# A four-layer graph network on one core: two small products after each group of four tiles in the first and fourth layer

## The chip, the cores and the metric

The kernel runs on one core of a Trainium2 chip. The metric is the device time of the whole kernel in microseconds. TensorE (PE in the profile, its weight loads PEld) multiplies matrices into PSUM; VectorE (DVE) and ScalarE (ACT) work on SBUF and PSUM; GpSimd (POOL) issues here almost only indirect DMAs, that is gathers of rows by index; SyncE (SP) issues the plain loads. The engines run side by side and wait for each other through semaphores.

## The reference

There are 12,500 nodes with 32 features and 400,000 edges, sorted by their destination. Each of four layers normalises the nodes, passes a message along each edge, sums the messages at the nodes and adds that to the features. The change touches the first layer (with a degree count of the third layer, which the kernel computes beside it) and the fourth:

```python
# first layer
m = relu(node_feat[src] + edge_feat)
neigh = segment_sum(m, dst)
return (1 + eps) * node_feat + neigh

# third layer's degree, counted beside the first
deg = segment_sum(ones(E), src)

# fourth layer
h = relu(edge_scalars @ fc_w1) * sqrt2
w = (h @ fc_w2).reshape(E, 4, 8, 8)          # 256 weights for each edge
x = node_features[src]
s1, v1, s2, v2 = x[:, :8], x[:, 8:].reshape(E, 8, 3), edge_sh[:, 0], edge_sh[:, 1:4]
out_s = A * (einsum('eu,euw->ew', s1 * s2, w[:, 0]) + c * einsum('eui,ei,euw->ew', v1, v2, w[:, 1]))
out_v = B * (einsum('eu,euw,ei->ewi', s1, w[:, 2], v2) + einsum('eui,euw->ewi', v1 * s2, w[:, 3]))
node_out = segment_sum(concat(out_s, out_v), dst)
```

## The kernel before

Edges are cut into tiles of 128. Four tiles (G = 4) make a group, four groups a chunk of 2048 edges (CT = 16 tiles), and there are 196 chunks, so 784 groups a layer. All loops over chunks are unrolled. A host-side check of the destinations (the flag `fast`) chooses between two programs; with these inputs the fast one runs, and only that one is spoken of here. The Tile framework places the semaphores: a tile of a pool with `bufs=n` waits until all that used the tile n before it in that pool has ended. It also sets each engine's order, so that an engine's instructions need not stand in the order of the source.

**First layer** (`layer0`, run by `edges`). For each group, POOL gathers four times 128 source rows (`gather`, L535), four groups ahead of their use, into six buffers `hs`. DVE adds the edge features (L663), ACT applies the relu (L664). Then `tail` does two things. `collect` builds a one-hot matrix of the destinations (DVE, L457) and multiplies it with the messages into one PSUM tile for the chunk (`ps_win`, PE, L460, f32: each product is two records in the profile); at the chunk's end ACT copies it out (L463) and stores it. And the degree is counted: the source index is split into a high and a low digit (DVE, L680 to L683), both become one-hot matrices `ohi` and `olo` in bf16 (DVE, L687, two buffers each), and PE multiplies them into `ps_deg` (L690, four products a group); at the chunk's end DVE adds that to `deg` (L693). DVE and ACT run their instructions in order, so a wait at L693 or L463 holds all that follows.

**Fourth layer** (`edges3`). Chunks are again pipelined. `gather` (POOL, L1274) fetches 16 times 128 rows a chunk, into four buffers `hs`, whose last reader is the multiply into `ps` (L1316) of the chunk's last group. `hidden` (PE, L1285, into the one buffer `ps_h`; ACT, L1287, relu into `hid`) makes the edges' hidden values for the next chunk, a quarter after each group. `product` is called once a group: eight f32 products (16 records) of `hid` with the weights `w2b` into `ps_w` (PE, L1310, two buffers), and then three multiplies on DVE that read `ps_w`: into `pa` (L1314), `ps` (L1316) and `pv` (L1318). Once a chunk DVE reduces them (`outputs`, L1326 to L1334) and splits the result in three bf16 parts with ACT (`thirds`, L472 to L476), PE sums them by one-hot matrices that ACT made (L1340, L1341; `collect`, L1346), and a product with `fold` (L1352) joins the parts.

PSUM pools of the fourth layer: `ps_h` with one buffer of 4 KB a partition, `ps_w` with two of 4 KB, `ps_sum` with one of 2 KB. Of the first: `ps_win` and `ps_deg`, two buffers each.

Of the kernel before, what the change touches and what calls it, by code (L numbers as in the profile page):

```python
# [8 lines left out]
F32 = mybir.dt.float32  # L9
# [5 lines left out]
PSUM = bass.MemoryType.PSUM  # L15

P = 128
D = 32
NP = 125
G = 4  # L20
# [17 lines left out]
def tiles_of(E):  # L38

    C = Q4 * B  # L40
    return E // C * (C // P) - (-(E % C) // P)
# [15 lines left out]
class GNN:  # L57
# [14 lines left out]
    def __init__(self, tc, ctx, a, out, E):  # L72
        self.tc, self.nc, self.ctx, self.a, self.out, self.E = tc, tc.nc, ctx, a, out, E
        self.N = a["x"].shape[0]
        self.J = self.N // NP
        self.T = a["src"].shape[1]
        self.CT = G * CG
        self.IT = self.CT * CPI0
        assert self.N % NP == 0 and self.T % self.IT == 0
        dram = ctx.enter_context(tc.tile_pool(name="dram", bufs=1, space=bass.MemoryType.DRAM))  # L80
        rows = self.N + P
        self.tabs = [
            [dram.tile([rows, D], F32, name=f"acc{l}_{k}", tag=f"acc{l}_{k}") for k in range(NTAB)]
            for l in range(4)
        ]
        self.feats = [dram.tile([rows, D], F32, name=f"feat{l}", tag=f"feat{l}") for l in range(4)]
        self.NW = self.T // self.CT
        self.real = tiles_of(E)


        self.emb8 = dram.tile([9, 8, self.NW, Q4 * B], BF16, name="emb8", tag="emb8")
        self.emb10 = dram.tile([9, 10, self.NW, Q4 * B], BF16, name="emb10", tag="emb10")
        self.mid = dram.tile([rows, D + 1], F32, name="mid", tag="mid")
        self.local = dram.tile([P, self.NW, self.CT + 1], F32, name="local", tag="local")
        self.n_e = dram.tile([P, self.T, 3], F32, name="n_e", tag="n_e")
        self.loc_t = dram.tile([self.NW, Q4 * B], F32, name="loc_t", tag="loc_t")
        self.n_t = dram.tile([4, self.NW, Q4 * B], F32, name="n_t", tag="n_t")
        self.dst_rows = dram.tile([P, self.T], I32, name="dst_rows", tag="dst_rows")
# [367 lines left out]
    def thirds(self, pool, c, step):  # L466
# [8 lines left out]
        else:  # L475
            nc.vector.tensor_tensor(c["f3"][:, :, 2, :], c["f"], c["f3"][:, :, 1, :], op=ALU.subtract)  # L476

    def get(self, pool, l, c):

        c["win"] = pool.tile([P, D], F32, name="win")  # L480
        self.nc.sync.dma_start(c["win"], self.feats[l][ds(self.first(c), P), :])
# [144 lines left out]
    def layer0(self):  # L626
        nc, tc, J = self.nc, self.tc, self.J
        if not self.fast:
            with tc.tile_pool(name="rest", bufs=1) as pool:
                for _ in self.rest(pool):  # L630
                    pass
        with ExitStack() as ctx:
            rest = None
            if self.fast:
                self.resident(ctx)
                rest = self.rest(ctx.enter_context(tc.tile_pool(name="rest", bufs=1)))
                for _ in range(TABS[0]):
                    next(rest)
            big = ctx.enter_context(tc.tile_pool(name="big0", bufs=LEAD + 4 if self.fast else 2))
            gp = ctx.enter_context(tc.tile_pool(name="gather0", bufs=AHEAD + 2))  # L640
            wp = ctx.enter_context(tc.tile_pool(name="work0", bufs=2))
            psum = ctx.enter_context(tc.tile_pool(name="psum0", bufs=2, space=PSUM))
            hist = ctx.enter_context(tc.tile_pool(name="hist0", bufs=2, space=PSUM))

            def load(col):
                if self.fast:
                    c = {"edge_attr_32": self.load(big, "edge_attr_32", col)}
                else:
                    c = {n: self.load(big, n, col) for n in ("src", "dst", "edge_attr_32")}
                    c["row"] = self.load_row(big, "dst_t", col)  # L650
                    c["rows"] = big.tile([P, self.CT], I32, name="rows")
                c["col"] = col
                return c

            def gather(c, t0):
                return self.gather(gp, "hs", 0, c["src"], t0, c)

            def front(c, t0, hs):
                return None

            def main(c, t0, hs, _):
                m = wp.tile([P, G, D], F32, name="m", bufs=3)
                nc.vector.tensor_add(m, hs, c["edge_attr_32"][:, t0 : t0 + G, :])  # L663
                nc.scalar.activation(m, m, AF.Relu)  # L664
                return m

            def tail(c, t0, m):
                if self.fast:
                    self.collect(0, wp, psum, c, m, t0)
                else:  # L670
                    eq = self.same(wp, c["dst"], c["row"], t0)
                    self.firsts(wp, eq, c["dst"], c["rows"], t0)
                    self.scatter(0, wp, psum, eq, m, c["rows"], t0)

                if t0 == 0:
                    c["deg"] = hist.tile([P, P], F32, name="ps_deg")
                hi = wp.tile([P, G], F32, name="hi")
                lo = wp.tile([P, G], F32, name="lo")
                s = c["src"][:, t0 : t0 + G]
                nc.vector.tensor_scalar(hi, s, -0.5 * (J - 1), 1.0 / J, op0=ALU.add, op1=ALU.mult)  # L680
                nc.vector.tensor_scalar_add(hi, hi, ROUND)
                nc.vector.tensor_scalar_add(hi, hi, -ROUND)
                nc.vector.scalar_tensor_tensor(lo, hi, -float(J), s, op0=ALU.mult, op1=ALU.add)  # L683
                ohi = wp.tile([P, G, NP], BF16, name="ohi")
                olo = wp.tile([P, G, J], BF16, name="olo")
                for oh, v, n in ((ohi, hi, NP), (olo, lo, J)):
                    nc.vector.tensor_tensor(oh, self.iota[:, None, :n].to_broadcast([P, G, n]),  # L687
                                            v[:, :, None].to_broadcast([P, G, n]), op=ALU.is_equal)
                for k in range(G):
                    nc.tensor.matmul(c["deg"][:NP, :J], lhsT=ohi[:, k, :], rhs=olo[:, k, :],  # L690
                                     start=t0 + k == 0, stop=t0 + k == self.CT - 1)
                if t0 + G == self.CT:
                    nc.vector.tensor_add(self.deg, self.deg, c["deg"][:NP, :J])  # L693
                    if not self.fast:
                        nc.scalar.dma_start(self.dst_rows[:, ds(c["col"], self.CT)], c["rows"])

            self.edges(load, gather, front, main, tail,
                       windowed=(lambda c, row: c.update(self.places_of(big, row), src=self.sources_of(c))) if self.fast else None, beside=rest)
        with tc.tile_pool(name="end0", bufs=1) as pool:
            agg = self.gather_sum(0, pool)  # L700
            nc.vector.tensor_add(self.x, self.x, agg)
            nc.vector.scalar_tensor_tensor(self.x, self.h, self.eps1, self.x, op0=ALU.mult, op1=ALU.add)
# [549 lines left out]
    def edges3(self):  # L1252

        nc, tc, CT = self.nc, self.tc, self.CT
        with ExitStack() as ctx:
# [3 lines left out]
            ph = ctx.enter_context(tc.tile_pool(name="ph3", bufs=1, space=PSUM))  # L1259
            pw = ctx.enter_context(tc.tile_pool(name="pw3", bufs=2, space=PSUM))  # L1260
            ps = ctx.enter_context(tc.tile_pool(name="ps3", bufs=1, space=PSUM))

            def fetch(c):
                row = c["no"]
# [25 lines left out]
            def scalars(c):  # L1290
# [7 lines left out]
                vv = c["vv"] = wp.tile([P, CT, 3, 8], F32, name="vv")  # L1298
                nc.vector.tensor_mul(vv.rearrange("p g i u -> p g (i u)"), hs[:, :, 8:32], sh[:, :, 0:1].to_broadcast([P, CT, 24]))

            def product(c, g):

                if g == 0:
# [4 lines left out]
                for k in range(4):  # L1308
                    for m in range(2):
                        nc.tensor.matmul(w[:, k, :], lhsT=c["hid"][:, m, 4 * g + k].rearrange("p q s -> p (q s)"), rhs=self.w2b[:, m, :],  # L1310
                                         start=m == 0, stop=m == 1)
                gs = slice(4 * g, 4 * g + 4)
                hs = c["hs"][:, gs, :]
                nc.vector.tensor_mul(c["pa"][:, gs], w[:, :, 0:128].rearrange("p g (w u) -> p g w u", u=16),  # L1314
# [3 lines left out]
                nc.vector.tensor_mul(c["pv"][:, gs].rearrange("p g i (w u) -> p (g i) w u", u=8),  # L1318
                                     w[:, :, None, 192:256].to_broadcast([P, 4, 3, 64]),
                                     c["vv"][:, gs].rearrange("p g i u -> p (g i) u")[:, :, None, :].to_broadcast([P, 12, 8, 8]))  # L1320

            def outputs(c):
                sh = c["sh"]
# [225 lines left out]
```

## Time and profile before

| what | us |
|---|---|
| time, median of 3 runs | 20938.48 (20915.86 to 20953.58) |
| the profiled execution's own time | 20931.77 |
| its span | 20930.0 |
| PE busy | 12599.4 (60%), 56,444 products and as many weight loads |
| DVE busy | 12740.1 (61%) |
| ACT busy | 6408.9 (31%) |
| POOL busy | 14745.9 (70%) |
| gathers of the first layer, from first to last | 72.3 to 4744.6 |
| gathers of the fourth layer, from first to last | 15396.3 to 20767.0 |

The four layers follow each other, with the second and third in one stage between the two that are changed. Busy shares over the whole span therefore mix stages with different limits; each stage has to be read by itself. A product's start in the profile is recorded, its end is modelled. When an instruction waited, the profile names what released it; "issue" is a wait for nothing that it shows, and "remote" one that a semaphore event ended beside which no instruction's end stands. The chain of work that ended last has 27% of the span on DVE, 20% on "issue", 15% on PE, 14% on POOL and 13% on "another core or an unknown queue", the chain's name for "remote".

### The profile page before, as it was taken

How to read it: one execution, taken by the hardware profiler on the slowest of the kernel's cores; microseconds unless marked ns; L12 is line 12 of the kernel's file. 1: busy time of each engine (PE TensorE's matmuls, PEld its weight loads, DVE VectorE, ACT ScalarE, POOL GpSimd, SP SyncE). 2: the span in 40 equal slices, each digit the busy share in tenths (PEclk: the TensorE clock that was granted, in tenths of full speed). 3: DMA queues.
4: the chain of work that ended last, by engine and by line, in shares of the span. 5: the costliest groups of instructions: out<-in, count | busy, mean ns of one | idle time of the engine just before them, and what ended most of it. 6: DMA issues, size and time to landing. Idle time of an engine off the chain costs nothing.

```text
span 20930.0 us, 189759 instructions
## 1 busy us (share of the span) xinstructions
PE 12599.4 (60%) x56444; PEld 6767.2 (32%) x56444; DVE 12740.1 (61%) x25505; ACT 6408.9 (31%) x13844; POOL 14745.9 (70%) x12508
## 2 busy tenths in 40 slices
PE   2443433334766666666666666666637777777776
PEld 2333433331211111111111111111125555555554
DVE  3554444334766666666666666666746666666666
ACT  0001110002333333333333333333324444444444
POOL 5777777774788888888888888888755555555553
PEclk9999999998777777777777777777768888888888
DMA  2113332112444444444444444444411111111111
GB/s 96 46 45 111 113 91 74 23 23 72 98 89 90 88 91 90 89 89 90 90 90 90 90 90 90 90 90 90 92 39 23 23 23 23 23 23 23 23 23 30
DMA packets 1482594, 1406.96 MB, mean 67 GB/s; under 512 B 1055751, under 2 KB 1250897, under 8 KB 1426409
## 3 DMA queue, kind: packets, MB, share of 16 engines
q1 hardware_dynamic: 668550, 1143.45, 17.2%
q0 software_dynamic: 750000, 205.60, 12.0%
q10 hardware_dynamic: 62992, 45.63, 0.7%
q8 instruction: 448, 7.34, 0.1%
q14 instruction: 604, 4.94, 0.1%
HBM read 1156.82 MB, written 236.20 MB: 67 GB/s over the span
## 4 chain that ended last, share of the span: by engine, by line
DVE 27%; issue 20%; PE 15%; POOL 14%; another core or an unknown queue 13%; ACT 7%; DMA 4%; DVEq 0%; ACTq 0%; SPq 0%; POOLq 0%
DVE z L853 6%; POOL acc L1008 5%; POOL hs L809 5%; PE ps_w L1310 5%; POOL hs L535 4%; PE ps_y L850 4%; DVE pv L1318 1%; DMA hs<-feat,src_all 1%; PE ps_o L860 1%; ACT oh L1340 1%; DVE f L1327 1%; DVE pa L1314 1%; ACT X L834 1%; PE ps_sum L1346 1%
## 5 line engine op out<-in xcount | busy, mean ns | idle before, releaser
L1008 POOL DMA_INDIRECT acc<-summed,rows x3125 | 5141.5, 1645 | 999.8 <-issue 882.0
L1274 POOL DMA_INDIRECT hs<-feat,src_all x3125 | 3017.6, 966 | 2462.6 <-DVE ps L1316 1460.3
L535 POOL DMA_INDIRECT hs<-feat,src_all x3125 | 3375.3, 1080 | 1368.4 <-issue 864.4
L809 POOL DMA_INDIRECT hs<-feat,src x3125 | 3210.6, 1027 | 1190.2 <-issue 944.4
L1310 PE MATMUL ps_w<-w2b,hid 128*128 128x256 f32 x12544 | 3194.7, 411 | 68.8 <-issue 53.4
L853 DVE TENSOR_TENSOR z<-ps_y,hid 128x1024 f32<-128x1024 f32 x2352 | 2837.7, 1214 | 411.2 <-PE ps_y L850 161.2
L850 PE MATMUL ps_y<-X,w2t 64*128 64x512 f32 x4704 | 2380.0, 744 | 1132.0 <-DVE z L853 656.2
L1310 PEld LDWEIGHTS ps_w<-w2b,hid 128*128 128x128 f32 x12544 | 2577.7, 209 | 625.8 <-issue 85.8
L850 PE MATMUL ps_y<-Q,w2t 64*128 64x512 f32 x4704 | 1677.6, 838 | 1678.1 <-DVE z L853 1163.8
L460 PE MATMUL ps_win<-m,oh 128*128 128x32 f32 x6272 | 1472.7, 400 | 854.9 <-ACT m L664 211.4
L472 ACT CAST f<-f 128x512 bf16<-128x512 f32 x784 | 481.2, 614 | 4785.3 <-DVE f L878 3878.6
L860 PE MATMUL ps_o<-z,sums 128*32 128x512 f32 x9408 | 1746.1, 700 | 30.0 <-DVE r L865 21.4
L460 PEld LDWEIGHTS ps_win<-m,oh 128*128 128x128 f32 x6272 | 1396.3, 328 | 927.7 <-issue 528.3
L690 PE MATMUL ps_deg<-olo,ohi 128*125 128x100 bf16 x3136 | 462.8, 298 | 2001.6 <-DVE olo L687 1416.9
L1287 ACT ACTIVATE hid<-ps_h 128x1024 f32<-128x1024 f32 x784 | 802.0, 1023 | 2368.0 <-remote 1923.5
L1314 DVE TENSOR_TENSOR pa<-ps_w,q 128x512 f32<-128x512 f32 x784 | 540.1, 689 | 1605.5 <-remote 1407.0
L824 DVE STREAM_TRANSPOSE X<-hs 128x512 f32<-128x512 f32 x392 | 273.4, 700 | 1999.8 <-DMA hs<-feat,src 1328.8
L850 PEld LDWEIGHTS ps_y<-Q,w2t 64*128 64x128 f32 x4704 | 521.2, 256 | 2923.8 <-DVE z L853 1578.9
L850 PEld LDWEIGHTS ps_y<-X,w2t 64*128 64x128 f32 x4704 | 614.2, 210 | 2343.2 <-DVE z L853 1159.5
L663 DVE TENSOR_TENSOR m<-hs,edge_attr 128x128 f32<-128x128 f32 x784 | 228.3, 291 | 1609.6 <-issue 779.8
L664 ACT ACTIVATE m<-m 128x128 f32<-128x128 f32 x784 | 240.3, 310 | 3145.1 <-DVE m L663 1175.9
L690 PEld LDWEIGHTS <-ohi 128*125 128x125 bf16 x3136 | 445.7, 215 | 1990.8 <-DVE ohi L687 1035.7
(207 smaller groups left out, 19667.1 us busy)
## 6 DMA issues: line engine op xcount, KB each, us to landing
has<-loc_t SPq DMA_DIRECT2D x392, 1024.0 KB
srow<-in_src_t SPq DMA_DIRECT2D x392, 512.0 KB
N<-n_t SPq DMA_DIRECT2D x3136, 32.0 KB
hs<-feat,src_all POOLq DMA_INDIRECT x6250
emb<-pp SPq DMA_DIRECT2D x252, 280.0 KB
emb<-emb SPq DMA_DIRECT2D x196, 360.0 KB
emb<-pp SPq DMA_DIRECT2D x252, 224.0 KB
emb<-emb SPq DMA_DIRECT2D x196, 288.0 KB
```

The costliest lines, as they stand in the source:

```text
L460: nc.tensor.matmul(c["sum"], lhsT=oh[:, k, :], rhs=feat[:, k, :], start=t0 + k == 0, stop=t0 + k == self.CT - 1)
L535: self.nc.gpsimd.indirect_dma_start(out=t[:, k, :], out_offset=None, in_=self.feats[l][:], in_offset=bass.IndirectOffsetOnAxis(ap=idx[:, t ...
L690: nc.tensor.matmul(c["deg"][:NP, :J], lhsT=ohi[:, k, :], rhs=olo[:, k, :], start=t0 + k == 0, stop=t0 + k == self.CT - 1)
L809: nc.gpsimd.indirect_dma_start(out=c["hs"][:, k, :], out_offset=None, in_=self.feats[1][:], in_offset=bass.IndirectOffsetOnAxis(ap=c["src" ...
L850: nc.tensor.matmul(y[:, q, :], lhsT=self.w2t[64 * q : 64 * q + 64, h, j, :], rhs=c["Q" if j < 3 else "X"][64 * q : 64 * q + 64, h, :], sta ...
L853: nc.vector.tensor_mul(z, y, c["hid"][:, 2 * h : 2 * h + 2, :])
L860: nc.tensor.matmul(c["o", j // 3][32 * q : 32 * q + 32, :], lhsT=self.sums[:, j, :], rhs=c["z", j, q % 2][:, q // 2, :], start=j % 3 == 0, ...
L1008: nc.gpsimd.indirect_dma_start(out=self.tabs[2][k % NTAB][:], out_offset=bass.IndirectOffsetOnAxis(ap=c["rows"][:, G * g + k : G * g + k + ...
L1274: nc.gpsimd.indirect_dma_start(out=c["hs"][:, k, :], out_offset=None, in_=self.feats[3][:], in_offset=bass.IndirectOffsetOnAxis(ap=c["src" ...
L1287: nc.scalar.activation(c["hid"][:, m, :, 2 * h : 2 * h + 2, :].rearrange("p b q s -> p q b s"), t.rearrange("p q (b s) -> p q b s", s=32), ...
L1310: nc.tensor.matmul(w[:, k, :], lhsT=c["hid"][:, m, 4 * g + k].rearrange("p q s -> p (q s)"), rhs=self.w2b[:, m, :], start=m == 0, stop=m == 1)
L1314: nc.vector.tensor_mul(c["pa"][:, gs], w[:, :, 0:128].rearrange("p g (w u) -> p g w u", u=16), c["q"][:, gs, None, :].to_broadcast([P, 4, ...
```

## The change

A new helper `settle` writes `settles` (2) products into a PSUM pool that has one buffer. Each product takes 128 x 32 weights and one moving column and gives a 32 x 1 result that nothing reads; each is its own tile. It is called once a group:

- in the first layer after the four degree products, with operands that these have just used (`ohi` and `olo` of the group's last tile, bf16);
- in the fourth layer after the group's eight products and ahead of the three multiplies that read them, with operands from `pv` of the group before (f32), which the multiply at L1318 wrote. The first group of the layer has none and no such products.

```diff
@@ -85,6 +85,7 @@
+        self.settles = 2
@@ -475,6 +476,12 @@
+    def settle(self, pool, lhsT, rhs):
+
+        for _ in range(self.settles):
+            t = pool.tile([D, 1], F32, name="ps_t")
+            self.nc.tensor.matmul(t, lhsT=lhsT, rhs=rhs, start=True, stop=True)
+
@@ -641,6 +648,7 @@ layer0
             hist = ctx.enter_context(tc.tile_pool(name="hist0", bufs=2, space=PSUM))
+            after = ctx.enter_context(tc.tile_pool(name="after0", bufs=1, space=PSUM))
@@ -689,6 +697,8 @@ layer0, tail
                     nc.tensor.matmul(c["deg"][:NP, :J], lhsT=ohi[:, k, :], rhs=olo[:, k, :],
                                      start=t0 + k == 0, stop=t0 + k == self.CT - 1)
+                if self.fast:
+                    self.settle(after, ohi[:, G - 1, :D], olo[:, G - 1, 0:1])
@@ -1259,6 +1269,7 @@ edges3
             ps = ctx.enter_context(tc.tile_pool(name="ps3", bufs=1, space=PSUM))
+            after = ctx.enter_context(tc.tile_pool(name="after3", bufs=1, space=PSUM))
@@ -1298,6 +1309,8 @@
+            state = []
+
             def product(c, g):
@@ -1309,6 +1322,8 @@
                         nc.tensor.matmul(w[:, k, :], lhsT=c["hid"][:, m, 4 * g + k].rearrange("p q s -> p (q s)"), rhs=self.w2b[:, m, :],
                                          start=m == 0, stop=m == 1)
+                if state:
+                    self.settle(after, *state)
@@ -1318,6 +1333,7 @@
                 nc.vector.tensor_mul(c["pv"][:, gs].rearrange("p g i (w u) -> p (g i) w u", u=8),
...
+                state[:] = c["pv"][:, 4 * g, 0, 0:D], c["pv"][:, 4 * g, 1, 0:1]
```

## The prediction

> **What bounds the kernel now.** I read the busy time by stage first, with stage edges taken from the first and last gather of each layer. In each row the pairs are busy time and instruction count of PE, PEld, DVE, ACT and POOL, then granted clock, DMA share, GB/s.
>
> ```profile
> 72.00:4780.00 4708.00, 1845.00 (x9408) 1783.08 (x9408) 2060.01 (x6784) 389.08 (x1106) 3375.28 (x3125) 1.00 0.25 68
> 4780.00:15300.00 10520.00, 6881.16 (x29392) 1927.00 (x29392) 7089.21 (x14140) 3507.96 (x7244) 8352.11 (x6250) 0.77 0.42 89
> 15300.00:20750.00 5450.00, 3796.19 (x17245) 2995.08 (x17246) 3452.75 (x4422) 2454.20 (x5373) 3009.15 (x3117) 0.83 0.12 24
> ```
>
> The first row is the first layer, the last row the fourth; the middle is not touched. In the fourth layer no engine is full: a chunk lasts 5450 / 196 = 27.8 us, PE works 19.4 of it, DVE 17.6, POOL 15.4. So it is bound by waits, and I looked at who waits there longest (total us, times, longest):
>
> ```profile
> ACT hid L1287 <- remote: 1914.6, 307, 41.1
> POOL hs L1274 <- DVE ps L1316: 1453.0, 191, 13.5
> DVE pa L1314 <- remote: 1398.9, 236, 34.4
> ```
>
> "remote" is a semaphore event beside which no instruction ends. On one core, pa and hid wait for nothing but PE's products, so these are products whose completion signal arrives long after the profile has them end. The order of time in one chunk shows it (start, us, what, idle time before):
>
> ```profile
> 18040.04 3.72 PE L1310 MATMUL ps_w<-w2b,hid 128*128 128x256 f32 x16 [0.54 <-issue]
> ...
> 18043.60 0.60 PE L1285 MATMUL ps_h<-emb,w1s 72*128 72x512 bf16 x2
> 18044.13 3.72 PE L1310 MATMUL ps_w<-w2b,hid 128*128 128x256 f32 x16
> ...
> 18050.13 0.95 POOL L1274 DMA_INDIRECT hs<-feat,src_all  x1 [0.30 <-issue]
> 18054.02 0.69 DVE L1314 TENSOR_TENSOR pa<-ps_w,q 128x512 f32<-128x512 f32 x1 [9.35 <-remote]
> 18054.06 1.02 ACT L1287 ACTIVATE hid<-ps_h 128x1024 f32<-128x1024 f32 x1 [10.19 <-remote]
> ...
> 18057.69 0.42 DVE L1316 TENSOR_TENSOR ps<-ps_w,hs 128x256 f32<-128x256 f32 x1
> ...
> 18058.38 0.94 POOL L1274 DMA_INDIRECT hs<-feat,src_all  x1 [7.30 <-DVE ps L1316]
> ```
>
> The group's product is over at 18043.76; its reader starts at 18054.02, three microseconds after the last of 16 gathers (1.25 us apart, the first at 18031.18) was issued. In the chunk before, the gathers start at 18003.35 and the same pa starts at 18026.30: 22.8 and 22.95 us after the burst's start. I read from this that while gathers are queued back to back, PE's completion signals are held, and that they come out when the gathers' transfers are through. That is inferred from rows; no view names the holder. Then DVE finishes the chunk, its last ps frees a gather buffer, the next burst starts, and the loop closes. **What PE ran ahead in the hold** (the second product above, 3.72 us) is what makes the end of the chunk short.
>
> The first layer is set by POOL (16 gathers at 1.25 us = 20 of a chunk's 23.8 us) and has the same holds:
>
> ```profile
> 1180.21 0.56 PE L690 MATMUL ps_deg<-olo,ohi 128*125 128x100 bf16 x4 [1.91 <-DVE olo L687]
> ...
> 1203.31 0.95 POOL L535 DMA_INDIRECT hs<-feat,src_all  x1 [0.30 <-issue]
> 1209.16 0.26 DVE L693 TENSOR_TENSOR deg<-deg,ps_deg 125x100 f32<-125x100 f32 x1 [28.17 <-remote]
> ...
> 1209.96 1.21 POOL L535 DMA_INDIRECT hs<-feat,src_all  x1 [5.70 <-DVE lo L683]
> ```
>
> PE has nothing to do from 1180.8 on, and the signal still takes until 1209.1: neither idleness of PE nor, as in the fourth layer, further products push it out.
>
> **The change part by part.** Nothing is removed. Added are 784 pairs of products in the first layer and 783 in the fourth (the first group has no operands yet).
>
> Products in the fourth layer. An f32 product is two records; the nearest small one is L1352:
>
> ```profile
> L1352 PE MATMUL ps_sum<-fold,s 96*128 96x32 f32 x392 | 87.1, 311 | 0.7 <-ACT s L1349 0.7
> L1352 PEld LDWEIGHTS ps_sum<-fold,s 96*128 96x128 f32 x392 | 91.2, 252 | 81.4 <-ACT s L1349 80.3
> ```
>
> Its two records take 0.41 us at 18031.10, so a pair that can't overlap takes 0.82 us, and 783 pairs 642 us. PE idles 5450 - 3796 = 1654 us there, so this is covered wherever PE would stand anyway; uncovered is the pair right ahead of a product that pa waits for.
>
> The waits. The first product of a pair needs pv of the group before; the next big product needs the same event for its PSUM buffer (two buffers), so this wait moves only what is queued between, hidden's L1285 and through it hid. The second product takes the buffer that the first one used. Nothing but PE touches it, so its wait is for **PE's own completion signal**: PE stands until its latest work is signalled. Behind it on PE are L1285 (ACT hid waits for that), the next group's L1310 (DVE pa) and L1346. No view of this trace shows PE waiting for itself; I infer it from the single buffer. With the signal prompt, this wait is inside the 0.82 us. In a hold, PE stands through it, and what it ran ahead today comes after the release: the next product, 3.72 us at full clock (5.37 us for the one at 18024.48), plus the pair.
>
> How often: 236 held waits of pa in 196 chunks, 5.93 us each on average (1398.9 / 236). In the two chunks read, the third group is held each time and the second in one. I take one exposed product a chunk, because the third group's hold is there in both: 196 x (3.72 + 0.82) = **890 us**. The upper end is all 236 held groups with the slower product: 236 x (5.37 + 0.82) = 1461 us. The lower end with no hold taken is the pair alone, once a chunk: 196 x 0.82 = 161 us. Below nothing: if the holds of pa went away, 161 - 1399 = -1238 us. I choose by the nearest row, the chunk above.
>
> The clock speaks for the upper part of this range: the chunk from 18003 to 18030, in which PE stood 6.3 us, was granted 0.79, that from 18031 to 18054 was granted 0.95. The Trainium skill, TensorE: Matmul & The Clock Gate, section Why this matters for your kernels, asks for no PE idle gaps over some 3 us, since the clock then falls back to half. By that rule the product after each release runs slow, and the term would be 196 x (5.37 + 0.82) = 1213 us in place of 890.
>
> The same page (The cost: per-tile semaphore tail) puts a signal at about 25 + 4.7 + 26.3 = 56 ns; an estimate from that is 3134 x 0.056 = 176 us for all added signals. The rows above, 9.35 and 28.17 us, say that here the signal is the dear part; I go by the rows.
>
> First layer. A bf16 product is one record; four of L690 take 0.56 us, a single one 0.30 us by its mean, so a pair that can't overlap takes 0.60 us, 470 us in all, covered by PE's 2863 us of idle time beside the gathers; without that cover it would cost all 470. The wait: in a hold PE no longer issues the next group's L460 and L690, so after the release 1.89 + 0.56 + 0.60 = 3.05 us pass before the group after it is signalled. DVE has work of its own for about that long (0.29 + 4 x 0.16 + 0.68 + 0.57 + 0.69 = 2.9 us a group), and ohi and olo (two buffers) now also wait for the pair that reads them. It counts where POOL stands for DVE:
>
> ```profile
> POOL hs L535 <- DVE lo L683: 205.0, 65, 6.9
> ...
> POOL hs L535 <- DVE hi L681: 68.1, 15, 7.9
> ```
>
> 80 such waits; with half of them exposed, 80 x 3.05 / 2 = **120 us**. The ends are 0 and one exposure a chunk, 196 x 3.05 = 598 us.
>
> No DMA is added but PE's code: 9400 records to the page's 112,888, fetched in 448 pieces so far, make 37 more; I put that at nothing, since the weight loads and products run on across fetches today, and at 37 x 1.3 us = 50 us (the fetches read took 1.2 to 1.35 us) if none were hidden. One more buffer for pv's reader costs nothing: it is read two chunks before it is written again.
>
> Sum: the profiled execution took 20931.8 us (span 20930.0); 20931.8 + 890 + 120 = 21942. The median of the runs shown lies 6.7 us above it, so **21,950 us**.
>
> **The rivals.** *The own wait isn't there, or never meets a hold:* then only the pairs' own time counts. PE's idle 8.4 us a chunk speaks for it, the 1.2 held groups a chunk against. 20938 + 161 = 21,100, and with all of it covered 20,940.
>
> *Two waits in a row meet the hold:* the next pair's first product also needs the last pair's second. If each held group costs one whole further hold, 236 x 5.93 = 1399, plus 161 and 120: 22,620. For it speaks that signals seem to leave in order; against it that all came at once when the gathers ended (18054.02 and 18054.06).
>
> *Faster:* PE held back at each group leaves fewer signals to be caught by the gathers, and pa's holds in the fourth layer go: 20938 - 1238 = 19,700. It decides as soon as a chunk sheds more than the pair's 0.82 us of its 1399 / 196 = 7.1 us of hold. Against it: the burst of gathers lasts 22.8 us whatever PE does, and in both traces above the signals stayed in with PE idle.
>
> **How the numbers follow.** Forecast 0.46, no own wait 0.23, two waits 0.17, faster 0.12; 0.02 for others. The likeliest gives 21,950; its own range is 21,400 to 22,500 (half of the two terms to one and a half). The range 20,960 to 22,650 takes in the second and third case but for what lies within no change, and leaves out faster. A measurement here can tell 0.2%, 42 us. Of the no-wait case 0.06 falls within that. Faster 0.12, same 0.06, slower 0.82.
>
> **What would show it.** Right: in the fourth layer's rows, the product after a held pa starts after the release and not before, pa's second wait in a chunk is for L1310, the chunk grows from 27.8 to some 32 us while the 16 gathers still take 20; the middle layers' 10520 us stay. The first layer grows by under 250 us. Wrong: PE's L1310 still runs twice within one hold (no own wait); or "remote" for pa falls well under 1399 us with a chunk under 27 us (faster); or the first layer grows more than the fourth.

## The result and the profile after

The changed kernel takes 21671.3 us (median of 4 runs, 21635.5 to 21691.0), the kernel before 20939.7 us (median of 4): a ratio of 1.0349, with a 95% interval from 1.0331 to 1.0367, or 732 us more. The profiled execution has a span of 21689.2 us.

The busy time by stage, with the stage edges put where they stood relative to the gathers in the profile before (columns as there):

```profile
72.00:4764.00 4692.00, 2041.27 (x10976) 1850.57 (x10976) 2072.54 (x6786) 387.39 (x1106) 3305.95 (x3125) 1.00 0.23 68
4764.00:15292.00 10528.00, 6911.80 (x29392) 1931.09 (x29392) 7092.55 (x14140) 3497.51 (x7244) 8340.60 (x6250) 0.77 0.41 89
15292.00:21506.00 6214.00, 4144.92 (x20276) 3129.19 (x20276) 3485.18 (x4422) 2414.75 (x5373) 3016.27 (x3120) 0.82 0.10 21
```

The first layer is 16 us shorter (4692 for 4708), the middle 8 us longer, the fourth layer 764 us longer: 6214 / 196 = 31.7 us a chunk in place of 27.8. In that stage PE works 349 us more and all other engines as much as before, so at least half of the 764 us, 415 us, is waiting. The waits of that stage (total us, times, longest):

```profile
POOL hs L1285 <- DVE ps L1331: 2209.1, 191, 18.6
...
DVE pa L1329 <- PE ps_w L1323: 1623.6, 380, 10.6
...
PE ps_t L483 <- remote: 1485.5, 147, 43.2
...
DVE pa L1329 <- remote: 567.4, 177, 37.0
```

`pa` waited 1398.9 us for held signals ("remote") before and waits 567 us for them now. But it now waits 1624 us, twice a chunk, for a product that really ends late, because PE itself stands at the small product `ps_t` (L483) for a signal. One chunk in order of time, cut to the third and fourth group:

```profile
18509.49 0.94 POOL L1285 DMA_INDIRECT hs<-feat,src_all  x1 [9.56 <-DVE ps L1331]
...
18518.63 0.22 PE L483 MATMUL ps_t<-pv 128*32 128x1 f32 x2
...
18518.79 0.70 PE L1323 MATMUL ps_w<-w2b,hid 128*128 128x256 f32 x2
...
18528.42 0.94 POOL L1285 DMA_INDIRECT hs<-feat,src_all  x1 [0.30 <-issue]
18530.83 0.18 PEld L483 LDWEIGHTS ps_t<-pv 128*32 128x32 f32 x2 [11.74 <-remote]
18530.83 0.27 PE L483 MATMUL ps_t<-pv 128*32 128x1 f32 x2 [11.34 <-remote]
...
18531.02 4.77 PE L1323 MATMUL ps_w<-w2b,hid 128*128 128x256 f32 x14
18535.83 0.69 DVE L1329 TENSOR_TENSOR pa<-ps_w,q 128x512 f32<-128x512 f32 x1 [7.76 <-PE ps_w L1323]
...
18536.31 0.70 PE L1323 MATMUL ps_w<-w2b,hid 128*128 128x256 f32 x2
...
18536.94 0.22 PE L483 MATMUL ps_t<-pv 128*32 128x1 f32 x2
...
18537.09 3.29 PE L1323 MATMUL ps_w<-w2b,hid 128*128 128x256 f32 x14
18540.42 0.69 DVE L1329 TENSOR_TENSOR pa<-ps_w,q 128x512 f32<-128x512 f32 x1 [1.23 <-PE ps_w L1323]
...
18541.71 0.94 POOL L1285 DMA_INDIRECT hs<-feat,src_all  x1 [12.35 <-DVE ps L1331]
```

The run of gathers starts at 18509.49. The third group's product gets two records off at 18518.79; then the order that Tile made puts the second small product, and PE stands at it for 11.34 us, until 21.3 us after the start of the run. The other 14 records, and the whole product of the fourth group, come only then; before the change the third one ran inside the hold, and in one of the two chunks that the prediction reads the fourth too. The next run of gathers waits for the last `ps` of this chunk and starts 32.2 us after the last one.

One correction to the text above: the flag `fast` is computed on the chip, not by the host, and both programs lie in the one kernel.

### The profile page after: what moved, and what is told of

Same layout as the page of the kernel before. It is cut to its first block, busy times and chain, and to the rows that moved or that the text cites. A ratio compares the mean times of both kernels' runs of the same rounds, so it can differ in the third digit from the quotient of the medians.

```text
span 21689.2 us, 199355 instructions
## 1 busy us (share of the span) xinstructions
PE 13190.0 (61%) x61144; PEld 6981.5 (32%) x61144; DVE 12788.5 (59%) x25505; ACT 6356.5 (29%) x13844; POOL 14668.8 (68%) x12508
## 4 chain that ended last, share of the span: by engine, by line
PE 33%; DVE 19%; another core or an unknown queue 17%; issue 14%; POOL 10%; ACT 4%; DMA 3%; DVEq 0%; ACTq 0%; SPq 0%; POOLq 0%
PE ps_w L1323 16%; DVE z L863 6%; PE ps_y L860 4%; POOL hs L819 4%; POOL acc L1018 4%; PE ps_win L461 4%; POOL hs L542 2%; PE ps_t L483 2%; PE ps_h L1296 2%; PE ps_o L870 1%; ACT X L844 1%; DVE cnt L1000 1%; DVE eq L995 1%; DVE summed L1014 1%
## 5 line engine op out<-in xcount | busy, mean ns | idle before, releaser
L1285 POOL DMA_INDIRECT hs<-feat,src_all x3125 | 3021.4, 967 | 3222.3 <-DVE ps L1331 2220.4
L542 POOL DMA_INDIRECT hs<-feat,src_all x3125 | 3306.0, 1058 | 1422.1 <-issue 877.0
L1323 PE MATMUL ps_w<-w2b,hid 128*128 128x256 f32 x12544 | 3530.6, 431 | 0.7 <-ACT hid L1298 0.7
L863 DVE TENSOR_TENSOR z<-ps_y,hid 128x1024 f32<-128x1024 f32 x2352 | 2836.3, 1213 | 454.3 <-PE ps_y L860 176.1
L1323 PEld LDWEIGHTS ps_w<-w2b,hid 128*128 128x128 f32 x12544 | 2574.3, 214 | 412.4 <-ACT hid L1298 1.1
L483 PE MATMUL ps_t<-olo,ohi 128*32 128x1 bf16 x1568 | 274.7, 175 | 2262.4 <-remote 1839.5
L483 PE MATMUL ps_t<-pv 128*32 128x1 f32 x3132 | 356.9, 183 | 1960.4 <-remote 1495.5
```

The source lines that it names most:

```text
L483: self.nc.tensor.matmul(t, lhsT=lhsT, rhs=rhs, start=True, stop=True)
L542: self.nc.gpsimd.indirect_dma_start(out=t[:, k, :], out_offset=None, in_=self.feats[l][:], in_offset=bass.IndirectOffsetOnAxis(ap=idx[:, t ...
L863: nc.vector.tensor_mul(z, y, c["hid"][:, 2 * h : 2 * h + 2, :])
L1285: nc.gpsimd.indirect_dma_start(out=c["hs"][:, k, :], out_offset=None, in_=self.feats[3][:], in_offset=bass.IndirectOffsetOnAxis(ap=c["src" ...
```

## The experiments

Three sets of four kernels were run, each on a chip of its own, with the kernel before on the same chip. That kernel took 20,943 us on the first chip, 20,796 us on the second and 18,944 us on the third, so only ratios within a set compare. The changed kernel itself was not run in these sets; its 21,671 us is set beside the first chip, where the kernel before took as long as beside it (20,943 and 20,940 us). The table gives the ratio with its 95% interval and the time of the fourth layer's gathers from first to last in the profiled execution (before: 5372 us, changed: 6135 us).

| kernel | chip | median us | ratio | fourth layer us |
|---|---|---|---|---|
| `l1_only` | 1 | 20,929 | 0.9991 (0.9982 to 1.0001) | 5387 |
| `l4_one_tile` | 1 | 21,277 | 1.0159 (1.0142 to 1.0177) | 5724 |
| `l4_single` | 1 | 21,170 | 1.0113 (1.0093 to 1.0133) | 5596 |
| `paced_before` | 1 | 21,390 | 1.0211 (1.0194 to 1.0228) | 5845 |
| `padded_before` | 2 | 20,636 | 0.9926 (0.9910 to 0.9943) | 5154 |
| `padded_after` | 2 | 20,616 | 0.9918 (0.9902 to 0.9935) | 5143 |
| `l4_one_long` | 2 | 21,358 | 1.0276 (1.0259 to 1.0293) | 5821 |
| `l4_one_four` | 2 | 21,152 | 1.0176 (1.0159 to 1.0193) | 5643 |
| `pad0_before` | 3 | 19,130 | 1.0099 (1.0083 to 1.0116) | 4168 |
| `pad256_before` | 3 | 19,619 | 1.0357 (1.0340 to 1.0374) | 4656 |
| `pad512_before` | 3 | 19,781 | 1.0439 (1.0421 to 1.0456) | 4816 |
| `pad256_after` | 3 | 19,636 | 1.0365 (1.0347 to 1.0382) | 4663 |

### Which layer

`l1_only` is the changed kernel without the pairs of the fourth layer:

```diff
-                if state:
-                    self.settle(after, *state)
```

> The pairs of small products stay in the first layer and are left out of the fourth. Theory A (the cost is the wait for PE's own held signal in the fourth layer): within 0.2% of before, 20,900 to 20,980 us; the first layer's gathers, from first to last, keep 4657 to 4675 us although PE stands some 1800 us there on its own signal. Rival B (each pair costs by itself, wherever it stands): half of the growth, 20,940 + 365 = 21,305 us. My recorded term for this layer would give 20,940 + 120 = 21,060 us.

0.9991: no difference. In the waits of its first layer PE stands at the pairs for held signals (total us, times, longest), and POOL, which sets that layer's end, still waits little for DVE:

```profile
PE ps_t L483 <- remote: 2028.2, 212, 38.0
...
POOL hs L542 <- DVE lo L691: 240.6, 59, 10.3
```

2028 us of standing cost nothing there; POOL's wait for `lo` grew from 205.0 to 240.6 us. All of the cost is in the fourth layer.

### Pair or wait

`l4_one_tile` has the same pairs, in the fourth layer alone, in one PSUM tile that is never given back (the lines that leave the pairs out of the first layer are not shown, here and below):

```diff
+            pair = after.tile([D, 2], F32, name="ps_t")
...
-                    self.settle(after, *state)
+                    for i in range(self.settles):
+                        nc.tensor.matmul(pair[:, i : i + 1], lhsT=state[0], rhs=state[1], start=True, stop=True)
```

> No pairs in the first layer; in the fourth the same 783 pairs with the same operands, but they write the two columns of one PSUM tile that is taken once and never given back, so neither of a pair waits for PE's own signal; the wait for DVE's pv stays. Theory A (own wait in a one-buffer pool, met by a held signal): 20,900 to 21,100 us, that is nothing up to one pair of 0.8 us a chunk (196 x 0.8 = 157), and the third product of a chunk runs inside the hold again. Rival B (the pairs' own PE time): 21,600 to 21,700 us as in the changed kernel. Rival C (PE waits for DVE's pv of the group before, and this is what pushes the product out): 21,600 to 21,700 us too, with PE's wait named as DVE pv.

`l4_single` has one small product a group in place of two, in the pool of one buffer, in the fourth layer alone:

```diff
-        self.settles = 2
+        self.settles = 1
```

> No small products in the first layer; in the fourth one product a group in place of two, still in a pool of one buffer, so that it waits only for the product of the group before. Theory A: a single product meets a hold one group later than a pair does, so the third product of a chunk is back inside the hold and only the fourth stands: 20,950 to 21,300 us, best 21,100. Rival B (PE time of the small products): half of the growth, 21,305 us, with the third product still inside. Rival D (any own wait meets the whole hold, however old the signal it waits for): 21,600 to 21,700 us.

`l4_one_tile` fell between the theories: 333 us (21,277 - 20,943), about half of the growth. Its timeline shows that the own wait is gone, and the third product is back inside the hold:

```profile
18507.39 0.94 POOL L1283 DMA_INDIRECT hs<-feat,src_all  x1 [14.03 <-DVE ps L1331]
...
18516.26 0.29 PE L1326 MATMUL ps_t<-pv 128*32 128x1 f32 x4
...
18516.47 3.72 PE L1322 MATMUL ps_w<-w2b,hid 128*128 128x256 f32 x16
...
18524.74 3.78 PE L1322 MATMUL ps_w<-w2b,hid 128*128 128x256 f32 x8
...
18529.49 0.19 PEld L1322 LDWEIGHTS ps_w<-w2b,hid 128*128 128x128 f32 x1 [0.43 <-issue]
18530.20 0.94 PEld L1322 LDWEIGHTS ps_w<-w2b,hid 128*128 128x128 f32 x5 [0.52 <-issue]
...
18530.33 0.69 DVE L1329 TENSOR_TENSOR pa<-ps_w,q 128x512 f32<-128x512 f32 x1 [5.04 <-remote]
```

The third product runs 9.1 us after the run of gathers starts, 16 records at once, and `pa` meets its signal when the hold ends at 22.9 us, as in the kernel before. But the fourth product is late, and after eight records at 18524.74 the next four come one by one, 0.71 us apart, with PE idle for "issue" (two of them are shown). `pa` waits longer for held signals than in the kernel before:

```profile
DVE pa L1329 <- remote: 1690.7, 280, 37.0
```

That is 284 us more than the 1407.0 us (237 times) of the kernel before in the same stage. So about 395 us of the change (21,671 - 21,277) need the pool of one buffer, and the other half needs only that small products stand between the big ones. The 395 us also take in a change of order on PE: in `l4_one_tile` the two small products stand together ahead of the big one, in the changed kernel two records of the big one stand between them. The wait for DVE's `pv` (rival C) is not it: at the pairs of that kernel PE's matmuls wait 25 us for it and its weight loads 135. `l4_single` at 21,170 us is inside the range of theory A and outside rival D's; it doesn't separate A from B.

To find what makes the second half, one long product took the place of the pair, and four small ones:

```diff
-            pair = after.tile([D, 2], F32, name="ps_t")
+            long = after.tile([D, 512], F32, name="ps_t")
...
-                    for i in range(self.settles):
-                        nc.tensor.matmul(pair[:, i : i + 1], lhsT=state[0], rhs=state[1], start=True, stop=True)
+                    o, n = state[0]["oh"], 4 * state[1]
+                    nc.tensor.matmul(long, lhsT=o[:, n, 0:D], rhs=o[:, n : n + 4, :].rearrange("p g e -> p (g e)"), start=True, stop=True)
...
-                state[:] = c["pv"][:, 4 * g, 0, 0:D], c["pv"][:, 4 * g, 1, 0:1]
+                state[:] = c, g
```

> In the fourth layer alone, and in one PSUM tile that is never given back, one bf16 product of 512 columns a group takes the place of the pair: two records on PE (a weight load and a matmul) in place of eight, with about the same time on PE; its operands are the one-hot rows oh that ACT has written, not DVE's pv. Theory H (in a hold PE goes on issuing until a certain number of its records is outstanding, and then one load and one matmul per 0.71 us, so that a record more ahead of the fourth product is what costs): about a quarter of the 333 us that pairs without own wait cost, 20,960 to 21,080 us. Rival I (the time on PE is what costs): 21,200 to 21,330 us.

```diff
-        self.settles = 2
+        self.settles = 4
...
-            pair = after.tile([D, 2], F32, name="ps_t")
+            pair = after.tile([D, 4], F32, name="ps_t")
```

> As the kernel with one PSUM tile that is never given back, in the fourth layer alone, but four small f32 products a group in place of two (16 records a group in place of 8), still no own wait. Theory H: the fourth product of a chunk meets the slow issue by 8 records earlier in each of the groups: another 250 to 500 us, 21,500 to 21,800 us. Rival I (time on PE): 4 x 0.15 us a group more, 196 x 4 x 0.29 = 227 us at most, 21,280 to 21,500 us. Rival J (the residue of 333 us has to do with the wait for pv and not with the products): 21,230 to 21,330 us, no growth.

Both expectations of theory H failed. Twice as many records cost no clear amount more (1.0176 against 1.0159, on another chip), and a quarter of the records cost more than the pair (1.0276). So neither the number of records nor their time on PE alone sets the cost. The long product is no clean test, since Tile put it ahead of `hidden` and so moved that too. What the second half goes by stays open. The 284 us more of held waits in `l4_one_tile` speak for the holds here too, but that is not shown.

### What makes the holds

`paced_before` is the kernel before with its four gather buffers kept as tiles, so that each four gathers wait for their own four tiles:

```diff
-            gp = ctx.enter_context(tc.tile_pool(name="gather3", bufs=4))
+            gp = ctx.enter_context(tc.tile_pool(name="gather3", bufs=1))
+            ring = [gp.tile([P, CT, D], F32, name=f"hs{i}") for i in range(4)]
...
-                c["hs"] = gp.tile([P, CT, D], F32, name="hs")
+                c["hs"] = ring[c["no"] % 4]
```

> The kernel before without any small products, but the four buffers hs of the fourth layer are taken once and used in turn, so that each four gathers wait for DVE's ps of their own four tiles and not all 16 for the last one: the gathers come in runs of four (5 us) spread over the chunk. If PE's completion signals are held while a long run of gathers is queued, short runs hold them for 5 to 8 us at most, pa's remote wait falls from 1399 us to under 700, and a chunk takes 20 to 25 us in place of 27.4: 19,450 to 20,450 us. If the holds have nothing to do with the length of the run (they go by the number of gathers, or come from something else), the total hold stays and the time is 20,800 to 21,100 us; if spread gathers reach more products than before, it is over 21,100 us.

It got slower (1.0211), and didn't do what it was meant to: DVE frees the groups 3.5 to 4 us apart, four gathers take 5 us, so a chunk's first 12 gathers still came in one run, and the last four some 2 us after the twelfth or at once. The run only began after the chunk's first group in place of its last, and another signal fell into it, that of `collect`'s product:

```profile
ACT s L1350 <- remote: 2573.8, 188, 16.3
```

13.7 us a time, in 188 of 196 chunks, with `fold` and the next chunk's products queued behind it on PE. So it matters which product's end meets the run.

`padded_before` and `padded_after` part the gathers by work of POOL's own, in the kernel before and in the changed one:

```diff
+            pause = ctx.enter_context(tc.tile_pool(name="pause3", bufs=1)).tile([P, 1024], F32, name="pause")
...
                 for k in self.rows_for(c["hs"], CT, c, 0):
+                    if k % 4 == 0:
+                        nc.gpsimd.memset(pause, 0.0)
+                        nc.gpsimd.tensor_copy(c["hs"][:, k : k + 4, :], pause[:, 0:128].rearrange("p (k d) -> p k d", k=4))
```

> The kernel before, without small products; ahead of every four gathers of the fourth layer POOL fills a scratch tile of 1024 floats and copies 128 of them into the rows that these gathers overwrite, so that runs of four gathers (5 us) are parted by about 1 us of POOL's own work. Theory F (the holds come from gathers that are issued faster, 1.25 us, than their transfers go, 1.43 us = 22.85 / 16, so that a backlog builds up over the run): the backlog of four gathers, 0.7 us, is worked off in each pause, the holds go, pa's remote wait falls from 1407 us to under 500, and a chunk takes 22 to 26 us, as the longer issue (16 x 1.25 + 4 = 24 us) allows: 19,600 to 20,700 us. Rival G (a hold lasts as long as any gathers run, whatever their rate): the run is 4 us longer and the holds with it, up to 196 x 4 = 784 us more: 21,300 to 21,750 us.

> The changed kernel (pairs in both layers, one PSUM buffer) with the same pauses between every four gathers of the fourth layer. Theory A with F: without holds PE's wait for its own signal is short, and what is left of the pairs is their PE time, up to 0.8 us for each pair of the chunk that stands ahead of a reader, 0 to 4 x 0.8 x 196 = 627 us over the padded kernel before; the added cost falls from 730 us to under 350. Rival G: 21,900 to 22,500 us. Rival B (the pairs cost by themselves): the distance to the padded kernel before stays at 700 to 780 us.

Both beat the kernel before on that chip, by 0.7 to 0.8%, and the distance between the two is gone: 20,616 against 20,636 us, where the change cost 732 us. (The changed kernel without pauses was not run on this chip; small products in the fourth layer cost 1.8 and 2.8% there.) POOL in `padded_before`, in a stretch with a slow copy (mostly it takes 0.29 us):

```profile
18511.73 0.98 POOL L1276 MEMSET pause<- 128x1024 f32 x1
18512.77 0.75 POOL L1277 COPY hs<-pause 128x128 f32<-128x128 f32 x1
18513.80 1.23 POOL L1278 DMA_INDIRECT hs<-feat,src_all  x1 [0.27 <-POOL hs L1277]
```

and the waits of its fourth layer (total us, times, longest), where `pa` in the kernel before, on the first chip, had 1398.9 us of "remote" in 236 waits and in `l4_one_long`, on this chip, 1450.9 us in 204:

```profile
DVE q L1297 <- DMA hs<-feat,src_all: 1031.3, 134, 9.3
...
DVE pa L1318 <- PE ps_w L1314: 56.3, 171, 0.5
...
DVE pa L1318 <- remote: 44.9, 2, 33.3
```

The holds are gone from this layer. They are still there in the first layer of the same execution, whose gathers have no pauses (685.1 us for `wsum`, below). Now POOL's 26.2 us (4 x 6.55) set the chunk, and DVE waits for gathers. In `padded_after` PE's wait at the pair for its own earlier signals went with them (same columns):

```profile
PE ps_t L483 <- DVE pv L1337: 804.2, 176, 6.7
...
PE ps_t L483 <- remote: 44.4, 2, 43.2
...
PEld ps_t L483 <- PE ps_t L483: 22.1, 81, 0.6
```

PE still stands 804 us at the pairs, but for DVE's `pv`, which comes when the gathers let it; behind that `pa` waits only 129 us for PE's products in the whole stage.

So PE's standing for late signals goes with the holds, and no cost is left. That both halves need holds is not shown by it: in `padded_before` PE stands 1339 us at L1314 for `pv`, 6.8 us a chunk, and the 422 us that PE works more in `padded_after` (4163 for 3742 in the layer) fit into that. What was wrong is theory F's picture of a backlog in the gathers' transfers. In the transfer records of the kernel before, a gather lands 2.0 to 2.1 us after its issue, at the third place of a run as at the sixteenth; the gathers themselves don't fall behind.

The third set was to find the shortest pause that keeps the holds away:

```diff
-            pause = ctx.enter_context(tc.tile_pool(name="pause3", bufs=1)).tile([P, 1024], F32, name="pause")
+            pause = ctx.enter_context(tc.tile_pool(name="pause3", bufs=1)).tile([P, 256], F32, name="pause")
```

(512 in `pad512_before`; in `pad0_before` the fill is made once, and only the copies stay.)

> The kernel before with the copy of 128 floats a group of four gathers but without the fill of 1024: in the padded kernel's trace four gathers with both take 6.55 us, the fill 0.96 and the step to the next instruction 0.07 of it, so that 4 gathers come in about 5.5 us, still faster than their transfers (4 x 1.43 = 5.72 us). Theory F (backlog): the backlog still grows over a run and the holds stay, pa's remote wait over 500 us; 0.98 to 1.03 of before. Rival K (not the rate helps but POOL's pause for its own signal between the gathers): the holds go as in the padded kernel, and as POOL needs only 22 us a chunk, the time falls to 0.955 to 0.975 of before.

> The kernel before with a fill of 256 floats in place of 1024: 6.55 - 0.96 x 3/4 = 5.83 us for four gathers, just slower than their transfers (5.72 us). Theory F: no holds (pa's remote wait under 300 us), and a chunk is set by POOL at 4 x 5.83 = 23.3 us in place of 26.3: 196 x 3 = 590 us less than with 1024, 0.962 to 0.972 of before. If the margin of 0.1 us is too small beside the other loads, the holds come back: 0.98 to 1.03.

> The same with a fill of 512: 6.55 - 0.48 = 6.07 us for four gathers, 24.3 us a chunk. Theory F: no holds, 196 x 2 = 390 us less than with 1024: 0.971 to 0.980 of before.

> The changed kernel (pairs in both layers, one PSUM buffer) with the fill of 256. Theory A with F: without holds the wait for PE's own signal is short, so the pairs add at most their PE time where POOL doesn't cover it; POOL's 23.3 us a chunk cover PE's 19.4 + 4 x 0.8 = 22.6 us: within 0.6% of the kernel before with the same fill, 0.960 to 0.978 of before. Rival B (the pairs cost 3.9 us a chunk by themselves, hidden in the other padded kernel by POOL's 26.2 us): 23.3 + 3.9 = 27.2 us a chunk, about 1.00 of before.

Three of the four ratios missed, because this chip took 18,944 us for the kernel before: it has no holds to take away. The fourth, 1.0099 for `pad0_before`, lies in theory F's range by luck, for F wanted holds and `pa` has no wait with a "remote" releaser there. So whether the pauses work by the length of the run, by the rate, or by POOL's wait for its own signal (rival K) stays untested. The first layer is the same code in `padded_before` on the second chip and in `pad0_before` on the third. The waits of ACT for `ps_win` there, on the second:

```profile
ACT wsum L463 <- remote: 685.1, 39, 38.9
```

and on the third:

```profile
ACT wsum L463 <- PE ps_win L460: 246.3, 92, 4.1
```

On the third chip no wait of the first layer has a "remote" releaser for `wsum` or `deg`, and its gathers take 4227 us in place of 4643 us from first to last, though POOL issues them 1.26 us apart (median) on both, on the third in longer runs (up to 834 without a gap of 2 us). Without holds the fourth layer is set by POOL alone: 21.3, 23.8 and 24.6 us a chunk for pauses without fill, with 256 and with 512 (22, 23.3 and 24.3 were expected). An estimate from that: the kernel before needs 18,944 - (19,127 - 4168) = 3985 us there for the fourth layer, 20.3 us a chunk, close to 16 gathers of 1.25 us. On this chip the pauses only lost.

`pad256_after` against `pad256_before` is the second comparison of the change without holds: 19,636 against 19,619 us, 0.1%. Rival B's 1.00 can't be read from the ratio to before. Its 3.9 us a chunk (764 us) don't show between these two, but that doesn't rule it out: PE stands 872 us at L1314 for `pv` in `pad256_before`, 4.5 us a chunk, which can cover them. The test would have been the changed kernel without pauses on the third chip; it was not run. Pauses under 1.4 us were not tried on the other two.

## Why the prediction was right, and where it was not

It said 21,950 us, 20,960 to 22,650, and slower with 0.82. Measured: 21,671 us. The signs that it named came: 31.7 us a chunk, a middle of 10,528 us, a product that starts after the release. That the total came so near is in part luck, as the terms show.

**The wait.** The prediction inferred from the single buffer that PE would wait for its own signal, which no view showed. The changed kernel shows it: 1485.5 us of PE at L483 in the fourth layer, 11.34 us in the chunk above, and the 14 records after the release as expected. In the trace the weight load that stands there waits for the semaphore that PE's own products count up. That settles the rival without such a wait. The rival of two holds in a row (22,620 us) didn't come either: the second product of the next pair starts at 18536.94, 0.63 us after the records ahead of it.

**The term of the fourth layer, 890 us, measured 764.** The mechanism stands for about half of it; the term was built wrongly in places that partly cancel. First, not one product a chunk is exposed but two: `pa` waits 380 times in 196 chunks for L1323. Second, PE is released before `pa` used to be: 21.3 us after the start of the run here, and 20.0 us in the median of the layer's runs, against the 22.8 and 22.95 us that the prediction read for `pa`. Third, the pool of one buffer accounts for only some 395 us; 333 us come from small products anywhere between the big ones, as `l4_one_tile` showed. The prediction had put 161 us on these, once a chunk, as PE time, with 0.82 us for a pair, where each small product takes 0.22 to 0.27 us in the rows above.

**The clock.** The prediction set 1213 us by the rule of the Trainium skill (TensorE: Matmul & The Clock Gate, Why this matters for your kernels) beside its 890. The rule's direction is in the trace. The granted clock in the 4.80 us after the wait of 11.34 us was 0.68, and 1.00 in the next product:

```profile
18531.00:18535.80 4.80, 4.80 (x17) 3.86 (x17) 0.00 (x0) 0.00 (x0) 0.00 (x0) 0.68 0.01 3
18537.10:18540.40 3.30, 3.30 (x20) 2.87 (x19) 1.98 (x4) 0.69 (x2) 0.00 (x0) 1.00 0.00 0
```

(columns as in the stages above). The 14 records took 4.77 us, and 3.29 us with the full clock. The term still lies under both estimates. In that chunk the earlier release (21.3 us for 22.8) gives back about the 1.5 us that the slow clock costs; that it does so everywhere is not shown.

**The first layer, 120 us, measured -16 us**, and `l1_only` at 0.9991. Here the step failed: it let half of POOL's waits for DVE grow by 3.05 us. In `l1_only` PE did stand 2028 us, but POOL's wait for `lo` grew by 36 us only. POOL runs four groups ahead, and what PE lost there was idle.

**The rival "faster"** had a true part: `pa`'s "remote" fell from 1398.9 to 567.4 us. The time came back as the wait for a product that is late. The test in the prediction ("well under 1399 us with a chunk under 27 us") needed its second half.

**What it took for granted:** that a run of gathers holds PE's signals until its transfers are through. That is so for only about half of the waits. In the first of its two chunks, whose run starts at 18003.35, a held signal came out while gathers were still being issued (the kernel before, columns as in the chunk above):

```profile
18020.49 0.69 DVE L1314 TENSOR_TENSOR pa<-ps_w,q 128x512 f32<-128x512 f32 x1 [7.21 <-remote]
18021.04 0.94 POOL L1274 DMA_INDIRECT hs<-feat,src_all  x1 [0.30 <-issue]
...
18022.28 0.98 POOL L1274 DMA_INDIRECT hs<-feat,src_all  x1 [0.31 <-issue]
```

Counted in that trace, of 194 waits of `pa` over 1.5 us in runs of 16, beside whose end no product ends, 105 end 22.5 to 23.2 us after the start of the run and 88 end 14 to 20 us after it. Such late signals are in the traces of two chips, and on the second breaking the run removes them; on the third no wait of the four kernels has a "remote" releaser. The changed kernel was not run there without pauses, so whether it would cost nothing is not shown. The prediction was for the chip whose trace it read.

## What to carry to other kernels

A tile in a pool of one buffer makes an engine wait for its own completion signal; that was short where signals were prompt (PE's weight loads stood 22 us for it in the whole layer of `padded_after`), and takes up the whole delay where they are late, so look in the trace how late that engine's signals come before adding one. If a wait shows a releaser beside which nothing ends, find out which other engine's stream is running at the time; breaking that stream is a cheap test and on one chip was worth 0.7%. Run such a test on more than one chip: what gained 0.7% on the second lost 1 to 4%, in other lengths, on the third.

## What was not expected of the hardware

- The kernel before differs by 10% between chips (20,943, 20,796 and 18,944 us). Part of the difference is in the first layer, whose gathers take 4673, 4643 and 4227 us on the three, 1.25 to 1.26 us apart; the fourth layer of the kernel before, 5372 us on the first chip, is put at some 3985 us on the third by the estimate above.
- On the first chip PE's completion signals come late beside a run of 16 gathers, some of them only about 22.8 us after its start; on the second chip they come late too (1450.9 us of waits of `pa` in `l4_one_long`). The gathers land 2.0 to 2.1 us after issue all along. With some 1.4 us of other work on POOL after each four gathers, two such waits of `pa` were left, 45 us in all. What holds the signals was not found.
- In `l4_one_tile` and `l4_one_four` PE's issue is slowed as well late in such a run, to one weight load and one matmul each 0.71 us (210 and 237 such steps in the layer, at most 28 in any other kernel looked at).
